# Unused products of zeros in TensorE's queue, in a two-layer graph network

## The chip, the cores and the metric

The kernel runs on one core of one Trainium2 chip. The metric is the device time of one execution in microseconds (us), taken as the median of the runs shown.

## What is computed

The reference takes 6250 nodes with 128 features and 200000 edges whose targets are sorted. It runs two graph layers, each behind a layer norm and a ReLU and each added to its input.

```
h = relu(layernorm(x))
x = x + attention2(elu(attention1(h)))      # 4 heads of 16, then 1 head of 128
h = relu(layernorm(x))
x = x + convolution(h, edge_attr_4, edge_attr_8)
```

An attention layer weighs the source row of every edge by a softmax over the edges of its target and sums these rows by target. The convolution, for every edge:

```
h = gelu(edge_scalar_attr @ W_mlp1 / sqrt(8))
h = gelu(h @ W_mlp2 / sqrt(64))
w = einsum('pxu,ex->epu', W_tp, h) / sqrt(64)    # 4 x 32 weights for each edge
m0 = w[:,0] * e0 * a0                            # e0, e1: features of the source
m1 = w[:,3] * sum_i(e1 * a1) / sqrt(3)           # a0, a1: from edge_attr
m2 = w[:,1] * e0 * a1;   m3 = w[:,2] * e1 * a0
agg = segment_sum([m0, m1, m2, m3], edge_dst) / sqrt(20)
```

Two small products of `agg` and of the node's own features then make the output.

## The kernel before

Nodes lie in 49 blocks of 128. The edges of a block are a window of 34 columns of 128 edges, and most loops go over a window in five groups: four of eight columns and one of two (`GROUPS`). Attention 1, attention 2 and the convolution run one after the other.

*Attention 1.* The first 31 blocks are summed from gathered rows, the other 18 in a dense way from counted edges, and the counts are also what attention 2 reads. The steps of the three kinds are interleaved in the order in which the Python code emits them. For a group of gathered columns, `attending` has GpSimd fetch a row for every edge (`gather`, line 308, one indirect DMA a column), and `attend` then makes the one-hot matrix of the targets on VectorE (line 317), multiplies the transposed one-hot by the node factors on TensorE (line 353, one product of 24 columns for each of the group's columns, into the PSUM tile `pe`), sums three parts of that on VectorE (line 355), weighs the rows and splits them into two halves (lines 324 and 325). A later step of TensorE scatters the group into the block's accumulator (line 370). The tile `pe` has one buffer (`ps_pe`, bufs=1). In TensorE's queue stand between these the counting products (line 755, evicted by ScalarE at 757, fed by VectorE at 744) and the dense ones (lines 876 and 882).

*Attention 2* runs dense products (line 1118) over all blocks.

*The convolution.* For each group `convolve` transposes the edge attributes (TensorE, line 1165; ScalarE copies them to SBUF at 1167), runs the first layer (line 1172, four products), a Gelu on ScalarE (1175), the second layer (1177, one product of 512 columns), another Gelu (1179), and the third product, which gives the weights `w` of the edges (1185, eight products of 128 columns into the PSUM tile `big`). VectorE and ScalarE form the messages from these and the gathered rows (lines 1196 to 1208), split them into two halves (324, 325), and TensorE scatters them into the accumulator (1214, eight products of 512 columns). The first-layer and second-layer tiles come from `small()`, a pool of two PSUM buffers, the third from `big()`, also two. Every block ends with two more small products (1224, 1229) and one DMA of its output.

All of this is emitted through a framework that adds every semaphore and orders the instructions of each engine by its own scheduler: on TensorE the transpose and the first layer of the next group stand ahead of the scatter of earlier ones. [...]A float32 product counts as two records in the profile, each with a weight load.

The lines that the change and the prediction touch, all on TensorE:

- 353, 355 and 370: `attend`, the group's product, its reader on VectorE, and its scatter
- 1165, 1172, 1177, 1185 and 1214: `convolve`, in the order of one group

## Time and profile before

| what | value |
|---|---|
| median of 3 runs | 6019.94 us (5944.17 to 6031.77) |
| the profiled execution | 6136.95 us, its span 6135.2 us |
| mean granted TensorE clock over the span | 0.724 of full speed |
| attention 1, where gathered rows, counts and dense blocks overlap | about 600 to 2400 us of the span |
| attention 2 | about 2450 to 3000 us |
| convolution | about 3040 to 6120 us |

The sums of the prediction are made against the profiled execution. In the profile's rows an engine is PE (TensorE products), PEld (its weight loads), DVE (VectorE), ACT (ScalarE), POOL (GpSimd) or SP (the engine that only issues DMAs); L1177 is line 1177 of the code; `small<-hid,wm_sb` is the tile written and those read. An arrow in a bracket names what ended an engine's wait, and "issue" is a wait for nothing that the profile shows. The ends of products are modelled, since products are pipelined.

### The profile page before, as it was taken

How to read it: one execution, taken by the hardware profiler on the slowest of the kernel's cores; microseconds unless marked ns; L12 is line 12 of the kernel's file. 1: busy time of each engine (PE TensorE's matmuls, PEld its weight loads, DVE VectorE, ACT ScalarE, POOL GpSimd, SP SyncE). 2: the span in 40 equal slices, each digit the busy share in tenths (PEclk: the TensorE clock that was granted, in tenths of full speed). 3: DMA queues.
4: the chain of work that ended last, by engine and by line, in shares of the span. 5: the costliest groups of instructions: out<-in, count | busy, mean ns of one | idle time of the engine just before them, and what ended most of it. 6: DMA issues, size and time to landing. Idle time of an engine off the chain costs nothing. (4 is left out here: it accounts for less than half of the span.)

```text
span 6135.2 us, 69889 instructions
## 1 busy us (share of the span) xinstructions
PE 3425.7 (56%) x23441; PEld 2683.7 (44%) x23442; DVE 3642.0 (59%) x6107; ACT 2978.4 (49%) x7370; POOL 2783.4 (45%) x2787
## 2 busy tenths in 40 slices
PE   3123555555555555799655555555655555655555
PEld 2013444454454444688534333333433333433333
DVE  4244655655665565788656565555655565556556
ACT  2012665665565566799634444334433433434434
POOL 1665545444544451000155555445555555545553
PEclk9999565666665566899867777667767667666667
DMA  3243434443443343444211111111111111111110
GB/s 86 63 115 85 119 111 115 117 115 111 125 123 113 108 129 122 171 163 154 89 42 42 40 40 41 38 40 40 42 41 42 40 41 41 39 38 42 39 40 25
DMA packets 338660, 480.00 MB, mean 78 GB/s; under 512 B 188987, under 2 KB 228555, under 8 KB 334306
## 3 DMA queue, kind: packets, MB, share of 16 engines
q1 hardware_dynamic: 186626, 232.52, 12.3%
q0 software_dynamic: 89072, 154.07, 10.7%
q10 hardware_dynamic: 62576, 88.69, 4.3%
q8 instruction: 191, 3.13, 0.2%
q14 instruction: 195, 1.60, 0.1%
HBM read 369.53 MB, written 105.48 MB: 77 GB/s over the span
## 5 line engine op out<-in xcount | busy, mean ns | idle before, releaser
L308 POOL DMA_INDIRECT G<-table,srcw x2720 | 2712.2, 997 | 2950.6 <-issue 989.7
L1214 PE MATMUL whole<-halves,ohr 128*128 128x512 f32 x1666 | 660.3, 556 | 255.6 <-DVE halves L325 228.1
L862 ACT ACTIVATE ramp<-erb,sel 128x256 bf16<-128x256 f32 x1764 | 758.4, 499 | 0.7 <-issue 0.3
L1177 PE MATMUL small<-hid,wm_sb 128*128 128x512 f32 (+1 forms) x490 | 335.3, 775 | 661.7 <-issue 467.2
L757 ACT CAST ca<-small 128x392 bf16<-128x392 f32 x784 | 349.3, 482 | 572.7 <-remote 383.5
L1214 PEld LDWEIGHTS whole<-halves,ohr 128*128 128x128 f32 x1666 | 433.9, 276 | 434.7 <-DVE halves L325 273.7
L325 DVE TENSOR_TENSOR halves<-mid,halves 128x1024 fp32r<-128x1024 f32 (+1 forms) x245 | 260.5, 1063 | 596.6 <-ACT halves L324 450.6
L1175 ACT ACTIVATE hid<-small 128x512 f32<-128x512 f32 (+1 forms) x245 | 135.6, 553 | 964.5 <-remote 579.4
L755 PE MATMUL small<-key,lo 128*128 128x98 bf16 x3136 | 333.5, 257 | 444.0 <-ACT ca L757 239.3
L1196 ACT ACTIVATE g<-G,a 128x128 f32<-128x128 f32 x1666 | 535.3, 394 | 17.9 <-DMA a<-in_edge_attr 8.3
L1185 PE MATMUL big<-wtp_sb,hid 64*128 64x128 f32 x3332 | 365.2, 356 | 221.7 <-issue 153.2
L1185 PEld LDWEIGHTS big<-wtp_sb,hid 64*128 64x128 f32 x3332 | 297.9, 247 | 412.3 <-issue 264.6
L1109 ACT ACTIVATE ramp<-small,sel 128x256 bf16<-128x256 f32 (+1 forms) x1225 | 447.8, 620 | 61.1 <-DVE up L1113 26.5
L755 PEld LDWEIGHTS <-lo 128*128 128x128 bf16 x3136 | 258.9, 127 | 481.6 <-issue 463.1
L325 DVE TENSOR_TENSOR halves<-big,halves 128x1024 fp32r<-128x1024 f32 (+1 forms) x245 | 259.3, 1058 | 354.2 <-ACT halves L324 175.9
L744 DVE TENSOR_TENSOR lo<-slots,turned 128x2048 bf16<-128x2048 bf16 x196 | 239.5, 1222 | 349.6 <-PE small L755 179.8
L1172 PE MATMUL small<-a8t,wm_sb 64*128 64x128 f32 (+1 forms) x1764 | 360.4, 355 | 96.4 <-issue 71.9
L882 PE MATMUL up<-rc,up 128*128 128x102 bf16 x3528 | 319.5, 264 | 165.9 <-DVE up L864 106.9
L1177 PEld LDWEIGHTS small<-hid,wm_sb 128*128 128x128 f32 x490 | 95.7, 241 | 719.5 <-issue 491.1
L1179 ACT ACTIVATE hid<-small 128x512 f32<-128x512 f32 (+1 forms) x245 | 135.8, 554 | 543.9 <-PE small L1177 284.1
L1172 PEld LDWEIGHTS small<-a8t,wm_sb 64*128 64x128 f32 (+1 forms) x1764 | 303.6, 251 | 169.9 <-issue 112.4
L370 PE MATMUL whole<-halves,ohr 128*128 128x136 f32 x1054 | 250.6, 387 | 218.3 <-issue 64.9
(273 smaller groups left out, 6596.2 us busy)
## 6 DMA issues: line engine op xcount, KB each, us to landing
counts<-ca ACTq DMA_DIRECT2D x196, 392.0 KB
ct<-counts SPq DMA_DIRECT2D x196, 392.0 KB
rc<-rhs SPq DMA_DIRECT2D x63, 717.5 KB
G<-table,srcw POOLq DMA_INDIRECT x2720
oht<-dlow SPq DMA_DIRECT2D x31, 1088.0 KB
ctc<-counts SPq DMA_DIRECT2D x504, 56.0 KB
a<-in_edge_attr SPq DMA_DIRECT2D x49, 136.0 KB
rhs<-rc SPq DMA_DIRECT2D x7, 717.5 KB
```

Of the source, the lines that this page charges most:

```text
L308: nc.gpsimd.indirect_dma_start(out=G[:, c, :], out_offset=None, in_=table, in_offset=bass.IndirectOffsetOnAxis(ap=idx[:, c:c + 1], axis=0))
L325: nc.vector.tensor_tensor(ms[1], m, ms[0], op=OP.subtract)
L755: nc.tensor.matmul(ps[:, k * NKEY:(k + 1) * NKEY], lo[:, a, :, r], ky[:, a, :, r], start=True, stop=True)
L757: nc.scalar.copy(ca[:, :, i * W:(i + WBANK) * W].rearrange("p h (k d) -> p h k d", d=W), ps[:, :WBANK * NKEY].rearrange("p (k h d) -> p h ...
L862: nc.scalar.activation(ramp[:, i, :n * P], erb[:, h, :n * P], AF.Relu, bias=sel1[:, h0 + i, h:h + 1], scale=STEEP)
L882: nc.tensor.matmul(ups[k][:, h], up[:, i, k * P:(k + 1) * P], by_head[:, i, :, h, :], start=h0 + i + h == 0, stop=h0 + i + h == NB + H1 - 2)
L1109: nc.scalar.activation(ramp[:, h, :n * P], pe[:, :n * P], AF.Relu, bias=sel2[:, h0 + h, :], scale=STEEP)
L1172: nc.tensor.matmul(ph[:, j * P:(j + 1) * P], wm1_sb[:n * NRAD, j, :], a8t[:n * NRAD, :], start=True, stop=True)
L1177: nc.tensor.matmul(ph[:, :npr * P], wm2_sb, hid1[:, :npr * P], start=True, stop=True)
L1185: nc.tensor.matmul(pw[:, c, :], hid2[half, j * P:(j + 1) * P], wtp_sb[half].rearrange("x p u -> x (p u)"), start=True, stop=True)
L1196: nc.scalar.activation(g0[:, c], G[:, c, :], AF.Copy, scale=a0[:, c, :])
L1214: nc.tensor.matmul(acc, oh[:, c, :], ms[:, c].rearrange("e s h i u -> e (s h i u)"), start=start and c == 0, stop=stop and c == n - 1)
```

## The change

A tile `nothing` of 128 x 512 zeros in bf16 is made once. A helper `keep_busy(ps, n)` has TensorE multiply it by itself n times, 512 columns wide, into a PSUM tile; each product starts and ends its own sum, so nothing is added up, and the tile is written anew by the product that follows. The helper is called at three places, always just ahead of the product that fills the same tile: in `attend` ahead of line 353 (six zeros for a group of eight columns, two for one of two), and in `convolve` ahead of 1177 and ahead of 1185 (three for a group of eight, one for one of two). The number is the ceiling of n x 6 / 8 or n x 3 / 8.

```diff
+    nothing = const.tile([P, 512], BF16, name="nothing")
+    nc.vector.memset(nothing, 0.0)
...
+    def keep_busy(ps, n):
+        for i in range(n):
+            nc.tensor.matmul(ps, nothing[:, :P], nothing[:, :ps.shape[1]], start=True, stop=True)
...
         pe = ps_pe.tile([P, 512], F32, tag="pe", name="pe")
+        keep_busy(pe, -(-n * 6 // SB))
         for c in range(n):
             nc.tensor.matmul(pe[:, c * 6 * H:(c + 1) * 6 * H], oht[:, c, :], pq, start=True, stop=True)
...
         ph = small()
+        keep_busy(ph, -(-n * 3 // SB))
         nc.tensor.matmul(ph[:, :npr * P], wm2_sb, hid1[:, :npr * P], start=True, stop=True)
...
         pw = big()
+        keep_busy(pw[:, :4, :].rearrange("p a b -> p (a b)"), -(-n * 3 // SB))
         for j in range(npr):
             for c in range(j, n, NPR):
```

## The prediction

> **What bounds the kernel now.** I read the page's busy shares first, then busy time and clock by stage, then the order of time inside one block of the convolution, then TensorE's busy time in steps of the clock's own period. The page:

> ```profile
> PE 3425.7 (56%) x23441; PEld 2683.7 (44%) x23442; DVE 3642.0 (59%) x6107; ACT 2978.4 (49%) x7370; POOL 2783.4 (45%) x2787
> ...
> PEclk9999565666665566899867777667767667666667
> ```

> No engine is full. The last row is the TensorE clock granted in each fortieth of the span, in tenths: it is near full speed only early and in attention 2 (slices 17 to 20). By stage, columns as in the page's first part, then clock and DMA; the first row is attention 1, the second the convolution:

> ```profile
> 600.00:2400.00 1800.00, 994.68 (x9172) 893.85 (x9171) 1092.27 (x1914) 1119.73 (x2748) 835.09 (x799) 0.62 0.40 116
> 3040.00:6120.00 3080.00, 1756.65 (x7766) 1181.41 (x7766) 1807.52 (x2632) 1232.67 (x2979) 1619.66 (x1659) 0.69 0.15 40
> ```

> The convolution is half the span, and TensorE's 1757 us and VectorE's 1808 us together exceed its 3080 us: the two mostly alternate. Why shows in TensorE's own order of time (start, length, what; the idle time before it in brackets):

> ```profile
> 4236.42 0.93 PE L1172 MATMUL small<-a8t,wm_sb 64*128 64x128 f32 x6
> 4238.04 1.13 PE L1177 MATMUL small<-hid,wm_sb 128*128 128x512 f32 x2 [0.69 <-ACT hid L1175]
> 4239.00 0.27 PE L1165 MATMUL small<-ident,a 128*64 128x128 f32 x1
> 4239.85 1.16 PE L1185 MATMUL big<-wtp_sb,hid 64*128 64x128 f32 x16 [0.58 <-issue]
> 4240.85 1.05 PE L1172 MATMUL small<-a8t,wm_sb 64*128 64x128 f32 x8
> 4242.50 2.12 PE L1214 MATMUL whole<-halves,ohr 128*128 128x512 f32 x8 [0.60 <-issue]
> ```

> Product, Gelu, product, Gelu, product is a chain. TensorE waits 0.69 us for the first Gelu and 0.58 us for the second (ScalarE's Gelu is 0.60 us)[...]. So the kernel is bound by latency along chains through TensorE, ScalarE and VectorE, and each product's own length counts in it. The list of waits says the same: ScalarE waited 251 us for L1172 and 284 us for L1177, VectorE 89 us for L1185.

> That length depends on the clock. TensorE alone in steps of 3.41 us (length of step, busy time, clock, DMA):

> ```profile
> 4207.83:4211.24 3.41, 3.41 (x11) 0.50 0.15 38
> 4211.24:4214.65 3.41, 2.04 (x18) 1.00 0.19 48
> 4214.65:4218.07 3.42, 1.98 (x13) 1.00 0.19 50
> 4218.07:4221.48 3.41, 0.00 (x0) 0.50 0.29 77
> ...
> 4228.31:4231.72 3.41, 2.72 (x7) 0.50 0.05 13
> 4231.72:4235.13 3.41, 3.41 (x21) 0.50 0.00 0
> 4235.13:4238.55 3.42, 2.73 (x13) 1.00 0.14 38
> ```

> The clock is 0.50 or 1.00 for a whole step. A slow step that was busy throughout is followed by a fast one; 2.72 us of 3.41 was not enough. A fast step stays fast with 2.04 us busy after it was reached and fell after 1.98 us. So at the slow clock TensorE must leave almost no gap; at the fast one it may idle about 40%.

> [...]No row here shows a bf16 product of 512 columns; eight of L1214's take 3.78 us cold and 2.12 us warm, 0.47 and 0.27 us each with the last one's tail[...]. [...]I take each zero product to hold back what stands behind it.

> **The change, part by part.**

> *Once:* a tile of 128 x 512 bf16 and one fill by VectorE. At start TensorE waits for loads; nothing to 1 us; I take nothing.

> *How many.* The convolution has 49 blocks of four groups of eight and one of two: three zeros before L1177 and three before L1185 for eight, one each for two, so 49 x (24 + 2) = 1274. Attention 1 has 31 such blocks on gathered rows: six for eight, two for two, 31 x 26 = 806. Each brings a weight load; that overlaps the product before, as the page's loads do. No DMA is added and no queue but TensorE's is touched.

> *Waits that move.* A zero product is now the first to write its PSUM tile, so it takes over the wait for the tile's release. For L1177 and L1185 the two buffers are free early. In attention 1 the tile `pe` has one buffer, and 48 times TensorE waited for VectorE's L355 to have read it (212 us in all): there the zeros can't fill the wait but come after it, ahead of L353, and behind them queue the scatter L370, the counting L755 and the dense products L876 and L882, with ScalarE's L757 and VectorE's L744 waiting for those.

> *What they cost in the convolution.* Three take 0.65 us warm, 1.28 us cold. Gaps of 0.69 and 0.58 us cover the warm ones but for 0.07 us; cold ones stick out by 0.6 and 0.7 us. Some gaps are longer (TensorE's idle time before L1177 is 661 us, 2.7 us a group); I take it that six in ten at L1177 and eight in ten at L1185 are short, and that 37% of groups stay cold: 196 x 0.37 x (0.6 x 0.6 + 0.8 x 0.7) = 67 us, 9 us for the warm ones, some 6 us for the groups of two: 82 us of TensorE's time. Bounds: nothing, if the scheduler puts them in the long gaps, and 196 x 1.3 = 255 us.

> *What they bring there.* A slow step such as the one with 2.72 us busy becomes full, so the next is fast. For a group of eight the products take, cold and warm: L1172 2.07 and 1.05 us, L1177 2.08 and 1.13, L1185 2.08 and 1.16, L1214 3.78 and 2.12: 10.0 against 5.5 us. With 1.3 us for the group of two, that is 49 x (4 x 4.55 + 1.3) = 955 us between all cold and all warm. A mean clock of 0.69 is 38% of time at full speed. Every block also has idle stretches that no zero reaches (after 4218.07 TensorE is idle for 10.5 us, waiting for ScalarE, and VectorE's turn takes 4 to 5 us), each of which takes the clock down again, so I take 63%, not all: 955 x 0.25 = 239 us less. The bounds are 38% and 90%.

> *Of both, on the path:* I take 0.8, because each product is awaited at once, less the stretches where all three engines stand still: -191 + 66 = **-125 us**.

> *Attention 1.* The zeros' time is 806 x 0.36 us (two thirds cold) = 290 us. L353's product is early: VectorE waited 8 us in all for it. TensorE idles 45% of this stage, VectorE 39%, ScalarE 38%, and the buffers between them give slack; I put a tenth on the path, +29 us; bounds 0 and 290. For the clock: 995 us busy at 24% full speed is some 1190 us all cold and 660 all warm; ten points more are -53 us, half on the path, -26 us. Sum **about 0**. Covered by the idle time of TensorE; without it all 290 us show.

> *Elsewhere:* attention 2 runs at 0.99 already and is not edited.

> Sum: 6136.95 us of the profiled execution (its span is 6135.2) - 130 = 6007 us. The median shown is 6019.94 us, 1.9% below that execution, so in the same proportion **5890 us**, -2.2%.

> **The rivals.**

> *Slower: zeros run cold ahead of real work.* Place: before L353 in attention 1, where the queue is mostly busy already, and the short cold gaps of the convolution. With half of the 290 us on the path, the clock unmoved, and 62% of the convolution's groups cold (158 us), profiled time rises by some 250 us: about **6260 us**. For it: attention 1 needs a full step to speed up and six cold zeros are 2.6 us of 3.41. It decides once more than about four tenths of attention 1's zeros reach the path while the convolution gains under ten points.

> *No change:* the idle stretches take the clock down as fast as the zeros bring it up. Seven points are -53 us on the path, paid for by the zeros: **6020 us**. For it: TensorE already warms up two or three times a block.

> *Much faster:* fast steps need only some 2 us busy, and if the zeros keep most of them above that, the clock holds at 90% in the convolution: 955 x 0.52 x 0.8 = -397 us, about **5640 us**. Against it: the idle stretches of 7 to 10 us.

> *The change doesn't do what it says:* products of zeros might not count as activity, or the scheduler, whose order on TensorE is already not the code's (L1165 of the next group stands before L1185), may put them elsewhere. Then only cost is left, between the first two rivals.

> **How the numbers follow.** Forecast 0.43 (own range 5780 to 5980), much faster 0.12, no change 0.22, slower 0.23 (6080 to 6300). About 2% is what a measurement of this kernel can tell from no change: below 5900 and above 6140. Of the forecast's 0.43 some 0.34 lie below 5900: faster 0.46, within 0.32 with the rest of the forecast and nearly all of no change, slower 0.22. The range is 5660 to 6150: it takes in most of the much faster case and the edge of the slower one.

> **What would show it.** Right: the convolution's clock near 0.8 and the whole span's at 0.79 or more, from 0.724; means of L1214, L1172 and L1177 lower; attention 1's length within 40 us of before. Wrong: clock below 0.74, or attention 1 longer by 100 us with L353's group busier, or the long waits of ScalarE for L1172 grown by the zeros in front of L1177.

## The result, and the profile after

| | before | after |
|---|---|---|
| median | 5982.06 us of 4 runs (5943.46 to 6031.77) | 6278.42 us of 4 runs (6268.57 to 6302.87) |
| ratio to before, 95% interval | | 1.0497 [1.039, 1.0603] |
| the profiled execution | 6136.95 us | 6268.57 us |
| mean granted clock | 0.724 | 0.723 |
| attention 1, first to last product of `attend` | 2246.5 us | 2294.1 us |
| attention 2 | 529.8 us | 530.4 us |
| convolution, first to last Gelu of the first layer | 3070.1 us | 3154.5 us |

The kernel became 5% slower where 2.2% less was forecast. Before has a fourth run here (5943.46 us), which moves its median from 6019.94 us. The two profiles show only 132 us of the 296 us between the medians, since the one of before was taken of an execution 2.6% above its median. The code moves down by the lines added: L353, L355, L1172, L1175, L1177, L1179, L1185, L1196 and L1214 of before are L361, L363, L1180, L1183, L1186, L1188, L1195, L1206 and L1224 of after.

The page of after, busy shares and the clock in fortieths of the span:

```profile
PE 3837.3 (61%) x25521; PEld 2773.9 (44%) x25522; DVE 3647.6 (58%) x6108; ACT 2998.4 (48%) x7370; POOL 2805.1 (45%) x2787
...
PEclk8555776766676666999777777777777777777777
```

and the stages of after (attention 1, then the convolution; columns as in the prediction):

```profile
600.00:2400.00 1800.00, 1068.58 (x9544) 868.88 (x9543) 1068.71 (x1885) 1091.06 (x2660) 840.78 (x804) 0.68 0.40 115
3087.00:6243.00 3156.00, 1996.56 (x9017) 1246.69 (x9018) 1804.38 (x2621) 1241.82 (x2976) 1642.40 (x1659) 0.73 0.15 39
```

The clock did rise, from 0.62 to 0.68 and from 0.69 to 0.73, and the stages still became longer: TensorE is busier and nobody else is. That the clock of the whole span stands still, 0.724 and 0.723, comes from the profile: it has no record of the clock ahead of 614 us in before and of 110 us in after, and shows 1.00 there. TensorE's products don't agree with that 1.00: the scatter of attention 1 (L370) takes 415 ns at the median in those 614 us of before, as it does later at 0.50, against 276 ns at 1.00. With 0.50 put for the time without a record the spans come to 0.67 and 0.71, an estimate from these figures. So "near full speed only early" in the prediction was no more than a missing record.

In the list of costliest groups of after (busy time, mean of one in ns, idle time before it):

```profile
L1224 PE MATMUL whole<-halves,ohr 128*128 128x512 f32 x1666 | 610.3, 519 | 194.4 <-DVE halves L327 174.9 <-DVE ohr L319 18.4 <-issue 1.1
L351 PE MATMUL pe<-nothing 128*128 128x512 bf16 x806 | 323.3, 530 | 286.2 <-DVE w L363 211.8 <-issue 71.4 <-DVE rr L803 1.4
L351 PE MATMUL small<-nothing 128*128 128x512 bf16 x637 | 237.4, 468 | 0.0
L351 PE MATMUL big<-nothing 128*128 128x512 bf16 x637 | 217.1, 419 | 0.0
```

The scatter's product fell from 556 to 519 ns. In attention 1 the zeros inherit the wait for VectorE's w, 212 us, as the prediction said. In the convolution they wait for nothing. So the parts that were forecast are all there, and the sum is not. GpSimd's list of waits in the convolution of after (total, times, longest):

```profile
POOL G L310 <- issue: 883.0, 1550, 9.5
POOL G L310 <- ACT g L1206: 480.3, 56, 16.2
```

It waits up to 16 us for ScalarE's `g` to release a buffer of gathered rows: here the gathers don't set the pace.

### The profile page after: what moved, and what is told of

It reads as the page before. It is cut to its first block, busy times and chain, and to the rows that moved or that the text cites. A ratio compares the mean times of both kernels' runs of the same rounds, so it can differ in the third digit from the quotient of the medians.

```text
span 6266.8 us, 73994 instructions
## 1 busy us (share of the span) xinstructions
PE 3837.3 (61%) x25521; PEld 2773.9 (44%) x25522; DVE 3647.6 (58%) x6108; ACT 2998.4 (48%) x7370; POOL 2805.1 (45%) x2787
## 4 chain that ended last, share of the span: by engine, by line
PE 25%; issue 9%; another core or an unknown queue 7%; ACT 6%; DVE 3%; POOL 0%; DMA 0%; ACTq 0%; DVEq 0%
PE whole L1224 7%; PE small L1180 4%; PE big L1195 4%; PE small L1186 4%; ACT halves L326 3%; PE small L351 2%; ACT g L1206 2%; PE big L351 1%; ACT hid L1188 1%; DVE halves L327 1%; PE small L1173 1%; ACT hid L1183 1%; PE small L1239 0%; DVE dot L1210 0%
## 5 line engine op out<-in xcount | busy, mean ns | idle before, releaser
L1224 PE MATMUL whole<-halves,ohr 128*128 128x512 f32 x1666 | 610.3, 519 | 194.4 <-DVE halves L327 174.9
L1186 PE MATMUL small<-hid,wm_sb 128*128 128x512 f32 (+1 forms) x490 | 312.5, 727 | 465.6 <-ACT hid L1183 233.9
L1224 PEld LDWEIGHTS whole<-halves,ohr 128*128 128x128 f32 x1666 | 399.5, 250 | 373.5 <-DVE halves L327 216.9
L763 PE MATMUL small<-key,lo 128*128 128x98 bf16 x3136 | 317.3, 246 | 392.7 <-ACT ca L765 199.4
L1206 ACT ACTIVATE g<-G,a 128x128 f32<-128x128 f32 x1666 | 537.9, 396 | 17.8 <-DMA G<-table,srcw 8.2
L1183 ACT ACTIVATE hid<-small 128x512 f32<-128x512 f32 (+1 forms) x245 | 135.9, 555 | 855.0 <-remote 498.8
L351 PE MATMUL pe<-nothing 128*128 128x512 bf16 x806 | 323.3, 530 | 286.2 <-DVE w L363 211.8
L1180 PE MATMUL small<-a8t,wm_sb 64*128 64x128 f32 (+1 forms) x1764 | 373.6, 364 | 199.0 <-issue 141.3
L1195 PE MATMUL big<-wtp_sb,hid 64*128 64x128 f32 x3332 | 335.4, 342 | 231.3 <-issue 120.7
L351 PEld LDWEIGHTS <-nothing 128*128 128x128 bf16 x2080 | 205.7, 113 | 579.9 <-issue 501.9
L1180 PEld LDWEIGHTS small<-a8t,wm_sb 64*128 64x128 f32 (+1 forms) x1764 | 315.5, 260 | 274.7 <-issue 182.7
L1195 PEld LDWEIGHTS big<-wtp_sb,hid 64*128 64x128 f32 x3332 | 280.6, 238 | 351.5 <-issue 180.0
L1188 ACT ACTIVATE hid<-small 128x512 f32<-128x512 f32 (+1 forms) x245 | 136.1, 555 | 588.0 <-PE small L1186 287.1
L890 PE MATMUL up<-rc,up 128*128 128x102 bf16 x3528 | 284.2, 248 | 119.4 <-DVE up L872 91.4
```

Of the source, the lines that this page charges most:

```text
L351: nc.tensor.matmul(ps, nothing[:, :P], nothing[:, :ps.shape[1]], start=True, stop=True)
L763: nc.tensor.matmul(ps[:, k * NKEY:(k + 1) * NKEY], lo[:, a, :, r], ky[:, a, :, r], start=True, stop=True)
L1180: nc.tensor.matmul(ph[:, j * P:(j + 1) * P], wm1_sb[:n * NRAD, j, :], a8t[:n * NRAD, :], start=True, stop=True)
L1186: nc.tensor.matmul(ph[:, :npr * P], wm2_sb, hid1[:, :npr * P], start=True, stop=True)
L1195: nc.tensor.matmul(pw[:, c, :], hid2[half, j * P:(j + 1) * P], wtp_sb[half].rearrange("x p u -> x (p u)"), start=True, stop=True)
L1206: nc.scalar.activation(g0[:, c], G[:, c, :], AF.Copy, scale=a0[:, c, :])
```

## The experiments

Each ratio is against runs of before that were taken together with it on the same chip. The runs met two levels of time for one and the same kernel before, about 4720 us and about 6100 us, the recorded pair belonging to the second. The chips that the results number 1 and 2 occur at both. Every run below says its level.

### Each place alone, thinner, and doubled, at 4720 us

Attention 1 alone, the convolution alone:

```diff
-        keep_busy(ph, -(-n * 3 // SB))
-        keep_busy(pw[:, :4, :].rearrange("p a b -> p (a b)"), -(-n * 3 // SB))
```

```diff
-        keep_busy(pe, -(-n * 6 // SB))
```

> The zeros of attention 1 alone; both places of the convolution are as before. Theory 1 (the zeros' own time in TensorE's queue is what costs, everywhere they stand): 806 zeros of 0.36 to 0.43 us are 290 to 350 us of TensorE time; if a third to a half reaches the path, +100 to +170 us, ratio 1.017 to 1.028. Theory 2 (the convolution is where the loss is, attention 1 has slack, as the prediction put it): 0 to +50 us, ratio up to 1.008. Theory 3 (it is the scheduler's new order of the other instructions, which differs most in attention 1): the loss is here, +200 us or more, and comes back when the zeros have no length but the order stays.

> The zeros of the convolution alone, at both places; attention 1 is as before. Theory 1: 1274 zeros of 0.22 to 0.43 us are 280 to 550 us; less what the faster clock gives back, +100 to +200 us, ratio 1.017 to 1.033. Theory 2: nearly all of the 5%, +250 us or more. Theory 3: the order in the convolution hardly changes, so 0 to +50 us. If the clock's gain as forecast were there and only attention 1 were wrong: below 1.0.

All three places, but two columns wide; and all three with twice the number (12, 6 and 6):

```diff
-            nc.tensor.matmul(ps, nothing[:, :P], nothing[:, :ps.shape[1]], start=True, stop=True)
+            nc.tensor.matmul(ps[:, :2], nothing[:, :P], nothing[:, :2], start=True, stop=True)
```

> All the zeros at all three places, but two columns wide in place of 512: the same number of instructions, waits and weight loads, nearly no length; the order of the other instructions stays that of the kernel before (98% of TensorE's in attention 1, all in the convolution). Theory 1 (their length costs): ratio 1.00 to 1.01 and the clock of before. If their number, weight loads or the waits that they move ahead cost: 1.02 or more. Theory 3 (order): 1.00.

> Twice as many zeros at each place (12, 6 and 6 for a group of eight). Theory 1: the loss at least doubles, since the added ones find still less idle time: ratio 1.10 or more, though the clock rises further (above 0.78 in the convolution). If the clock's gain needed a certain number of zeros to set in (the forecast's mechanism with too small a dose): ratio below the 1.05 of the single dose and a clock near 0.9.

The change itself again, and before with the line numbers of after (the change without its three uses of `keep_busy`):

> The changed kernel once more, beside the kernel before. The earlier runs of parts of the change stood on a chip where the kernel before takes 4724 us and not 5982. If the 5% belongs to the change wherever it runs: 1.04 to 1.06 again, although its two halves alone gave 1.0074 and 0.9995. If the loss depends on how long TensorE's products take to be reported as done (the 7 to 10 us stretches in which all engines but GpSimd stand still, which the quicker executions don't have): 1.005 to 1.010 where the kernel before takes some 4720 us, and 1.04 to 1.06 where it takes some 6000.

> The changed kernel with its three calls taken out, which leaves the kernel before and an unused tile: a profile of it on this chip. If the difference between chips is a wait for TensorE: its convolution takes either 63 us a block, with 5 us and more between the end of L1172's last product and the Gelu in every second group of a block, or 44 us, with none, and the other engines' instructions last as long in both.

| run | median, us | ratio | clock of the span |
|---|---|---|---|
| attention 1 alone (e1) | 4763.11 | 1.0074 [1.0053, 1.0094] | 0.792 |
| convolution alone (e2) | 4721.29 | 0.9995 [0.9987, 1.0004] | 0.847 |
| two columns wide (e3) | 4726.77 | 1.0008 [0.9998, 1.0018] | 0.799 |
| doubled (e4) | 4770.55 | 1.0088 [1.0067, 1.011] | 0.878 |
| the change (f1) | 4763.27 | 1.0077 [1.0057, 1.0098] | 0.841 |
| before (f2, one run) | 4718.95 | | 0.800 |

The clock of the span again counts the time ahead of the first record as 1.00, some 510 us where attention 1 has no wide products (e2, e3, f2) and 110 to 130 us where it has, so this column doesn't compare kernels; the stages below do.

At this level the change costs 0.8%, all of it in attention 1: its last product comes at 1908.6 us (f1) in place of 1871.8 (f2). There the length of the products matters, since two columns cost next to nothing (1.0008, e3), but the cost is not in proportion to it: with twice as many (e4) the last product comes at 1913.6 us. The convolution is indifferent. Its stage in before (f2), then in the change (f1):

```profile
2600.00:4600.00 2000.00, 1465.04 (x7222) 986.99 (x7221) 1661.27 (x2444) 1147.43 (x2765) 1531.38 (x1538) 0.82 0.20 57
```

```profile
2600.00:4600.00 2000.00, 1536.62 (x8228) 980.74 (x8360) 1654.51 (x2437) 1180.40 (x2755) 1532.11 (x1536) 0.91 0.20 57
```

The clock rises from 0.82 to 0.91 (f1), and GpSimd issues 1538 gathers in these 2000 us before and 1536 after. GpSimd's own list of waits in this stage of the change (f1; total, times, longest) says why:

```profile
POOL G L310 <- issue: 401.1, 1316, 0.3
POOL G L310 <- DMA G<-table,srcw: 43.9, 144, 0.3
```

It never waits longer than 0.3 us, and before (f2) is the same in this:

```profile
POOL G L310 <- issue: 384.9, 1263, 0.3
```

It issues one gather after another, 1.25 us from start to start, and 34 of them make 42.5 of a block's 44.2 us. The chain that ended last in the change (f1), followed back from the end, is led by the same line:

```profile
POOL 19%; DMA 9%; issue 8%; PE 5%; ACT 4%; DVE 3%; POOLq 0%; DVEq 0%; ACTq 0%
```

The higher clock brings nothing there (0.9995, e2). In before (f2) TensorE's share of that chain, 13%, is above GpSimd's 10%, so the two ways are of nearly one length. The thin products leave the clock at 0.81 in the convolution (0.82 without any), where the wide ones take it to 0.91: products of zeros raised it here, and only the wide ones. The stage with thin products (e3):

```profile
2600.00:4600.00 2000.00, 1509.53 (x8363) 1042.44 (x8363) 1655.75 (x2442) 1147.62 (x2760) 1530.62 (x1541) 0.81 0.20 58
```

### The convolution without its gathers, at 4720 us

```diff
-            G = gath.tile([P, SB, D], F32, tag="G", name="G")
-            gather(G, table3, srcw[:, b, cs], n)
+            G = fixed
```

with `fixed` gathered once ahead of the loop, so that one group's rows serve for all groups and every other group's rows are left out; without any added products (g1, k3) and with the convolution's (g2, k4), twice, on two chips.

> Left out: the convolution's gathers of table3; one group's rows are gathered once and used for all groups, and there are no added products. Theory (GpSimd's gathers pace a convolution block at 44.1 us on the chips where the kernel before takes 4720 us, VectorE is next): without them a block takes what VectorE's 83% of it and its waits need, 37 to 41 us, and the kernel about 4720 - 49 x 5 = 4480 us, ratio 0.935 to 0.965. Rival (the chain through TensorE, ScalarE and VectorE sets the block, the gathers are covered): within 1% of before. If the chip is one where before takes about 6000 us, and the late reports of TensorE's products come with the gathers: the block falls from 64 us to 40 us as well and the time by some 1100 us; if the reports are late for another reason, the block stays above 55 us.

> As the run without gathers and without added products, with the added products at the convolution's two layers alone. Theory (a TensorE that is off the path): within 0.3% of that run, although the granted clock in the convolution rises from about 0.82 to 0.9. Rival 1 (the clock counts once the gathers do not pace the block): at least 1% under that run, that is 1 us a block. Rival 2 (the added products stand in the chain of the group once nothing covers them): at least 1% over that run.

> Left out: the convolution's gathers of table3, of which one group's rows serve all groups; no added products. On a chip of about 6000 us, if the late reports of TensorE's products come with GpSimd's gathers: a block of 40 to 43 us in place of 63 and about 1000 us less, ratio 0.80 to 0.86. If they come from TensorE itself or from the chip: a block over 55 us, ratio over 0.92. On a chip of 4720 us: 0.96, a block of 40.9 us, as before.

> As the run without gathers, with the added products of the convolution. If the clock's gain counts wherever gathers do not pace the block, 1 to 2% under that run on any chip (it was 68 us under it, a block of 39.6 us against 40.9); if that was a matter of the chip of that run, within 0.5% of it, or over it.

| | without added products | with the convolution's |
|---|---|---|
| first time (g1, g2) | 4560.37 us, 0.9638 [0.9609, 0.9667] | 4491.86 us, 0.9485 [0.9452, 0.9519] |
| second time (k3, k4) | 4555.12 us, 0.9641 [0.9625, 0.9658] | 4488.81 us, 0.9496 [0.9478, 0.9513] |
| median block of the convolution | 40.9 us | 39.6 us |

The stage without added products (g1), then with them (g2):

```profile
2600.00:4400.00 1800.00, 1336.16 (x6984) 906.80 (x6985) 1609.34 (x2374) 1094.32 (x2682) 0.00 (x0) 0.86 0.03 7
```

```profile
2600.00:4400.00 1800.00, 1515.47 (x8237) 978.89 (x8372) 1652.38 (x2441) 1145.44 (x2755) 0.00 (x0) 0.91 0.03 8
```

With GpSimd's column empty the same added products gain 68.5 and 66.3 us, 1.3 us a block, and TensorE's other products (the time covered by their records in the convolution) lost 70 us (g1, g2). So the mechanism of the forecast is real: a busier TensorE runs at a higher clock (0.91 for 0.86), and the chain of a group gets shorter, by those 1.3 us a block (thin products were not tried without gathers). In the real kernel it is not that chain that sets the block. The first rival of g2's expectation is the one that held.

### The other level: attention 1

```diff
-        keep_busy(pe, -(-n * 6 // SB))
+        keep_busy(pe, -(-n * 3 // SB))        # h1
+        keep_busy(small(), -(-n * 6 // SB))   # h2
```

without added products in the convolution.

> Three added products a group in attention 1 in place of six, none in the convolution. Six cost 35 us there (ratio 1.0074), twelve about 42 us. Theory 1 (the added products' own length stands ahead of the group's products): half of it, 15 to 20 us, ratio 1.003 to 1.0045, attention 1 ends 15 to 20 us after the 1872 us of before. Theory 2 (that they are in the queue at all moves the planner's order and with it the work of the other engines, whatever their length): 25 to 37 us, ratio 1.005 to 1.008. Theory 3 (three are covered, from six on they are not): within 0.1% of before.

> Six added products a group in attention 1, none in the convolution, written into a bank of the pool small and not into the bank pe that the group's own products use, so that they need not wait until VectorE's w of the group before has read pe. Theory 1 (the loss is the six products that start only when pe is free and stand between that and the group's products): most of the 35 us goes, ratio 0.999 to 1.002. Theory 2 (the order or the length on TensorE as such): 1.005 to 1.010. Theory 3 (the bank of small is taken from the counting's transposes and sums): over 1.010.

These two met the level of 6100 us: 1.0102 [1.0071, 1.0133] (h1) and 1.0123 [1.0072, 1.0175] (h2). The sizes expected had been put for the other level, so they decide little: half the products still cost 62 us, and the loss doesn't go away when they need not wait for `pe`. They did place attention 1 in the 5%: about 1.2 points of it.

### The other level: the convolution

Three more runs of the convolution alone and one of the thin products, meant for this level, met 4720 us:

> The added products of the convolution alone, a second time, in the hope of a chip on which the kernel before takes about 6000 us (as in the recorded pair and in the two runs before this one) and not 4720 us (as in the six first). Theory 1 (on such a chip the added products of the convolution make up what attention 1 leaves of the 5%: 5% less 1.2%): ratio 1.025 to 1.04. Theory 2 (the convolution is as indifferent there as on the other chips, and the 5% are attention 1 and the choice of the chip): 0.995 to 1.01. On a chip of 4720 us: 0.998 to 1.001, as before.

> All added products, each two columns wide. On a chip of about 6000 us: if the number of instructions on TensorE's queue or their order costs the time, 1.03 or more; if it is the length of the 512 columns, 0.99 to 1.01. On a chip of 4720 us: 0.999 to 1.002, as before.

> The added products of the convolution alone, for a chip on which the kernel before takes about 6000 us. Theory 1 (there they make up what attention 1 leaves of the 5%): 1.025 to 1.04. Theory 2 (indifferent there too): 0.995 to 1.01. On a chip of 4720 us 0.998 to 1.001 once more.

> As the run before: the added products of the convolution alone. On a chip of about 6000 us, theory 1: 1.025 to 1.04, theory 2: 0.995 to 1.01; on a chip of 4720 us: 0.998 to 1.001.

They gave 1.0 [0.9988, 1.0013] (k1), 1.0011 [0.9998, 1.0024] (k2), 1.0003 [0.9994, 1.0011] (m1) and 0.9991 [0.9983, 0.9999] (m2): the first part of the study again. The last two runs met 6100 us: h2's attention 1 together with the change's convolution, and all places with products two columns wide.

> Six added products a group in attention 1, written into a bank of the pool small in place of pe, and the added products of the convolution as in the change. At 4720 us for before (where the convolution's are worth nothing, ratio 0.999 to 1.000): what stays is attention 1. If its loss is the six products' place between the release of pe and the group's own products, 0.999 to 1.003; if it is their length or the order wherever they write, 1.005 to 1.010. At about 6000 us for before (where the same products in attention 1 alone gave 1.0123): if the convolution's make up the rest of the 5%, 1.035 to 1.055; if they are indifferent there too, 1.008 to 1.016.

> All the added products at all their places, each two columns wide. Where before takes about 6000 us and the change costs 5%: if the length of the 512 columns on TensorE costs it, 0.99 to 1.01; if number and order of the instructions on TensorE's queue do, 1.03 or more. At 4720 us: 0.999 to 1.002, as twice before.

The first took 6401.33 us, 1.05 [1.0437, 1.0563]: the 5% of the recorded pair, of which attention 1 alone had made 1.2 points, so the convolution's products cost 3.8 points, some 230 us, with intervals of about half a point on each of the two. The second took 6468.92 us, 1.0595 [1.0542, 1.0647]. Products of two columns, 165 ns each in the records, cost *more* than those of 512. In the thin run (q1), the zeros' tile, with duration in ns as least, median and most:

```profile
L351 PE MATMUL big<-nothing x637: 163/163/231, 3048.4 to 6432.2; 128*128 128x2 bf16 x160
L351 PE MATMUL small<-nothing x637: 163/167/187, 3084.7 to 6425.8; 128*128 128x2 bf16 x160
```

So at this level it is not the length of the products that costs, but that they stand in TensorE's queue. It is not a new order either: in the thin run TensorE's other products of the convolution come in exactly the order of before (in after one step a block has moved). In attention 1 the length doesn't decide either: from first to last product it takes 2295.8 us with thin products (q1) and 2294.1 with wide ones (after), against 2246.5. How, a stretch of the thin run's order of time shows (start, length, engine; in brackets the idle time before):

```profile
4329.26 1.12 PE L1186 MATMUL small<-hid,wm_sb 128*128 128x512 f32 x2 [2.20 <-ACT hid L1183]
...
4330.22 0.22 PE L351 MATMUL big<-nothing 128*128 128x2 bf16 x3
...
4330.30 0.27 PE L1173 MATMUL small<-ident,a 128*16 128x128 f32 x1
4339.89 0.60 ACT L1188 ACTIVATE hid<-small 128x512 f32<-128x512 f32 x1 [10.40 <-remote]
...
4340.54 2.08 PE L1195 MATMUL big<-wtp_sb,hid 64*128 64x128 f32 x16 [9.98 <-ACT hid L1188]
```

The second layer's product (L1186) ends at 4330.4 us by its record. Its Gelu (L1188) starts at 4339.89, and TensorE, which needs that Gelu, does nothing meanwhile. In between TensorE, VectorE and ScalarE all stand still while GpSimd goes on issuing gathers. TensorE's semaphore update, which the Gelu waits for, is in the trace at 4339.87. That is 9.5 us after the product's recorded end. At 4720 us there is no such delay: wherever ScalarE stood idle, this Gelu follows 0.04 us after the recorded end (k2). How an update comes about that much later than the recorded end is not shown.

The table adds up all stretches of over 2 us in the convolution in which these three engines stand still. Of those in before, after, n1 and q1, between 91 and 100% end within 0.05 us behind an update from TensorE.

| run | level | added products in the convolution | clock in a stretch of it | its length, us | standing still: stretches, us |
|---|---|---|---|---|---|
| f2 | 4720 | none | 0.82 | 2155.3 | 0, 0 |
| f1 | 4720 | 512 columns | 0.91 | 2162.1 | 1, 2 |
| k2 | 4720 | 2 columns | 0.81 | 2163.9 | 0, 0 |
| h1 | 6100 | none | 0.69 | 3040.5 | 73, 382 |
| h2 | 6100 | none | 0.70 | 3022.2 | 77, 403 |
| n1 | 6100 | 512 columns | 0.73 | 3229.7 | 122, 567 |
| q1 | 6100 | 2 columns | 0.68 | 3337.9 | 134, 646 |
| before | 6100 | none | 0.69 | 3070.1 | 80, 430 |
| after | 6100 | 512 columns | 0.73 | 3154.5 | 92, 409 |

Against the mean of h1 and h2 (3031 us, 393 us still), n1 is 198 us longer and stands still for 174 us more, q1 307 and 253 us. That is most of the loss. Wide products lose less than thin ones, 108 us less; the clock, 0.73 against 0.68, is in their favour, but that it makes the 108 us is not shown. In the chain that ended last, what comes from no work the profile knows is 15% in the thin run (q1) and 14% in n1, where after has 7%; the chains of before, h1 and h2 reach back over less than a fifth of the span and can't be set beside them. The thin run's:

```profile
PE 20%; another core or an unknown queue 15%; ACT 8%; issue 6%; DVE 3%; POOL 0%; DMA 0%; ACTq 0%; DVEq 0%
```

The recorded pair's own two profiles don't show more standing still by this count, 430 and 409 us. With stretches from 1 us up they do: 110 stretches and 471 us in before, 173 and 520 us in after, of which 101 and 167 end within 0.05 us behind TensorE's update. These 49 us are over half of the 84 us that the convolution grew between the two profiles. By the same count n1 stands still 193 us longer than h1 and h2 (442 us), and q1 272 us. The execution of before in the pair was a long one, so I take n1 against h1 and h2 as the better comparison, though they weren't taken together.

What stays open: why TensorE's completions come late at one level, and why more of its instructions make them come late more often. Attention 2, which has no gathers, has no such stretch in before and took 530 us at both levels. A link to the gathers is in the traces: while they are issued in the convolution of before, 53% of TensorE's updates fall between 0.625 and 1.0 us after a gather's start, where an even spread over the step of 1.25 us would give 30%, and at 4720 us (f2) it is 34%. How the one makes the other is not shown. Whether the standing still would vanish at 6100 us without gathers is not shown, since k3 and k4 met the other level. Number and place of the added products were not told apart, nor was the wait for `pe` at 4720 us.

## Why the prediction was wrong

**The step that failed** is "Of both, on the path: I take 0.8, because each product is awaited at once, less the stretches where all three engines stand still". It took eight tenths of what TensorE's products gain or cost as the convolution's own, and the standing still as something that the change leaves alone. At 4720 us the share on the path was 0: GpSimd's gathers set the block there, and the stage took 2162.1 us (f1) for 2155.3 (f2), though TensorE's other products lost 140 us. With the gathers gone the time fell by 68.5 us where those products lost 70 (g1, g2): there the share was nearly one, above the 0.8. At 6100 us the term put at nothing decided: the stretches of standing still grew, and the convolution became 198 us longer, 174 of them standing still (n1 against h1 and h2).

**A term was also sized wrongly.** The clock was to take 239 us off TensorE's products in the convolution. It took 57 us: the time that the records of all products but the zeros cover went from 1756.7 us in before to 1699.1 in after. That fits the share of time at full speed, which rose from 38% to 46% and not to 63%: 8 points of 955 us are 76 us. The added products' own records, 237 + 217 us, are no measure of their cost, since they overlap: in after a zero lasts 0.38 us by its record at full speed (0.63 us at half speed), but the next starts after 0.216 us (0.426 us), at the median. That is the price that the prediction used, 0.65 and 1.28 us for three: there it was the author's estimate, which no row of before showed, and after bears it out.

**Behind it is a line misread.** The prediction said that TensorE is idle for 10.5 us after 4218.07 "waiting for ScalarE". The order of time of before at that place:

```profile
4216.82 1.16 PE L1172 MATMUL small<-a8t,wm_sb 64*128 64x128 f32 x8 [1.28 <-issue]
...
4219.11 1.21 DVE L317 TENSOR_TENSOR ohr<-kept,dstw 128x1024 fp32r<-128x1024 f32 x1
...
4226.61 0.94 POOL L308 DMA_INDIRECT G<-table,srcw  x1 [0.30 <-issue]
4227.80 0.60 ACT L1175 ACTIVATE hid<-small 128x512 f32<-128x512 f32 x1 [10.08 <-remote]
```

ScalarE wasn't late; it had waited 10.08 us itself, and for TensorE: the update that let it go is in the trace at 4227.77, 9.8 us after the product's recorded end. Some 430 us of the convolution were of this kind. I took them off the share on the path as stretches in which nothing moves, and didn't ask whether TensorE's own queue makes them. That the Gelu's wait was "remote" and not for the product was in the page of before:

```profile
L1175 ACT ACTIVATE hid<-small 128x512 f32<-128x512 f32 (+1 forms) x245 | 135.6, 553 | 964.5 <-remote 579.4
```

Another reading was loose too: that TensorE's 1757 us and VectorE's 1808 us exceed a stage of 3080 us means that they overlap for at least 485 us, not that they alternate.

**The clock in the convolution.** At 4720 us the share of time at full speed went from 64% (a clock of 0.82) to 82% (0.91), 18 points of the 25 that were forecast; at 6100 us it went from 38% to 46%. The rule read from single steps of 3.41 us holds over the whole trace of before: of 210 slow steps in which TensorE was busy throughout, 183 were followed by a fast one, and of 609 with less than 2.7 us busy none; of fast steps, 302 of 304 with 2.3 us or more kept the speed and none of 142 with less than 1.5. What was overestimated is how many slow steps the zeros would fill. In the convolution of before 317 slow steps had less than 2.7 us busy, and in after still 295; at 4720 us they went from 53 (f2) to 6 (f1). Stretches such as the 10.5 us after 4218.07 are what the added products could not fill. Nor does it take an idle step to lose the speed: of those 142 fast steps of before 122 had some work in them, and the one from 4201.00 to 4204.41 us, with 1.43 us busy, was followed by one at 0.50.

**Attention 1.** A tenth of the zeros' time on the path, 29 us, was about right at 4720 us: 35 us of what is on record as

```profile
L351 PE MATMUL pe<-nothing 128*128 128x512 bf16 x692 | 264.0, 485 | 116.7 <-DVE w L363 104.5 <-issue 7.4 <-DVE rr L803 2.6
```

in the run with attention 1 alone (e1; some records are missing, 806 x 485 ns is 391 us, and the records overlap). That it came out near is in part luck, since doubling the zeros (e4) added only 5 us and the cost is therefore no fixed part of their time. The gain from the clock, forecast at 26 us, isn't seen: the clock there rose from 0.66 to 0.77 in the change at that level, and the stage still ended 37 us later. At 6100 us the stage's products cost 62 (h1) to 80 us (h2). So the sum "about 0" should have been a loss.

**The sum and the rivals.** The sum took -130 us from parts of -125 and about 0, which changes nothing. The slower rival gave 6260 us, on the scale of the medians, and 6278.42 came, but not by its mechanism, so that the number is luck: it had the clock unmoved and half of attention 1's zeros on the path. The clock moved, and by n1 and h2 three quarters of the loss are the convolution's. Of "the change doesn't do what it says", that zeros might not count as activity is refuted by the clock, 0.91 with wide products against 0.81 with thin ones; that the scheduler puts them elsewhere is in part true (zeros for the third product stand ahead of the second layer's), and it didn't decide. The one rival that mattered was missing: that another engine, GpSimd, sets the block, and that at the recorded level completions of TensorE do.

## What to carry to other kernels

Before a product of TensorE is made faster, ask what sets the period of the loop: an engine that never waits longer than its own issue (here GpSimd, 0.3 us, with 34 gathers of 1.25 us a block) left a clock of 0.91 for 0.82 without worth, and taking the gathers away for one run showed what the clock would be worth. Where a consumer's wait has no work behind it in the profile, while its producer's record has long ended, look for the producer's semaphore update: here it came 9.5 us (q1) and 9.8 us (before) late, and more instructions in the producer's queue made such stretches more frequent, 134 for 73 and 77, though they were only two columns wide. Filler products should be tried thin as well as wide: only that tells what their length costs from what their presence costs.
